# A graph layer and an attention layer on one core: transpositions behind the scalings, block sums on another engine

## The chip, the core and the metric

The kernel runs on one core of one Trainium2 chip. Times are device microseconds (us) of one execution. Engines: PE is TensorE's matmul, PEld its weight load, DVE VectorE, ACT ScalarE, POOL GpSimd, SP the engine that issues most transfers. The granted clock is the share of its full clock that TensorE was given, 1.00 being all of it. L690 is line 690 of the kernel; its code is below.

A *group* is four of the 128 batches. I measure a group from the first matmul of line 720 (attention times V) in it to the first one in the next group. Group 0 has no such matmul ahead of it; there I count from its first score matmul. Group lengths, landings and start times that are given without a fence are read from the trace's single records at these marks.

## The reference, cut to what matters

```python
x, adj: (128, 128, 512), (128, 128), float32
# layer 0
h = relu(layernorm(x))
x = x + relu(max along the row of (adj @ h) + b)  # one number per row, added to x
# layer 1
h = relu(layernorm(x))
q, k, v = h @ Wq + bq, h @ Wk + bk, h @ Wv + bv   # 512x512 weights, 8 heads of 64
weights = softmax(q k^T / 8 + mask(adj))
x = x + weights @ v
```

The kernel forms the q, k and v products by a scheme with fewer multiplications, in two levels. It needs sums of blocks of the weights (once) and of the transposed h (per group).

## The kernel before

The kernel keeps every matmul result in one of eight banks of PSUM. The parts that the argument touches (cuts marked `...`):

```python
def blocks(m):                    # DVE: 32x32 transpositions of batch m
    nc.vector.transpose(TB[g][:, :, i % 2], HN[m]...)            # L318
def move(m):                      # 16 transfers bring two batches' blocks to their place in hT
    for a in range(NQ):
        for q in range(NQ):
            nc.sync.dma_start(HT[g][...], TB[g][...])            # L328
def weight_blocks(eng, n):        # 16 sums of 128x128 blocks of weight n
    for k in (3, 2, 0, 1): ...
        eng.tensor_tensor(o, x, y, op=op)                        # L401

def scores(g):                    # 64 matmuls into all eight banks, in order
    for i in range(G):
        psc = [bank(2 * i + j)... for j in range(2)]
        for f in range(NC):
            for j in range(2):
                nc.tensor.matmul(psc[j][:, f, :], KT[g]..., QT[g]...)   # L690
        ... exp on ScalarE

def apply(g, n_last=G):           # attention times V, then the scalings
    for i in range(G):
        if i % n_last == 0:
            last = bank(7 if i == 0 else 0)      # head 7 of all four batches
        main = bank(3 + i)                       # heads 0 to 6 of batch i
        ... matmuls                              # L720
    for po, rs, oo in parts:                     # five parts: banks 3, 4, 5, 6, then 7
        nc.vector.reciprocal(rs, po[:, :, HD])                   # L737
        nc.vector.tensor_tensor(oo, po[:, :, 0:HD], rs..., op=ALU.mult)   # L738, "the scalings"

for g in range(NG):
    if g > 0:
        apply(g - 1)
    scores(g)
    part = [...]      # 18 steps: six each for the products v of group g, q and k of g + 1
    ...
    if g > 0:
        for i in range(G):
            residual(b - G + i, nc.gpsimd)       # L750, then the store
    ...               # norms of the group after next
    if g == 1: weight_blocks(nc.vector, "v")
    ...
    # in step 5: h_sum(g + 1, k), DVE differences of hT (L367), the first to read the moved blocks
    # in step 17: blocks(m + 2), blocks(m + 3), move(m + 3), the group's last two batches
    if g == 0: weight_blocks(nc.vector, "k")
```

The matmuls of `apply` fill banks 3 to 7, the scalings read them, and `scores` overwrites them a moment later.

Of the kernel before, what the change touches and what calls it, by code (L numbers as in the profile page):

```python
# [169 lines left out]
def tile_adj_preln_d2(  # L170
# [13 lines left out]
    nc = tc.nc  # L184
# [24 lines left out]
    def fast(ctx):  # L209
# [103 lines left out]
        def blocks(m):  # L313

            g, i = divmod(m, G)
            if i % 2 == 0:
                TB[g] = proj.tile([P, NQ, 2, NC, Q], F32, name="tb")
            nc.vector.transpose(  # L318
                TB[g][:, :, i % 2], HN[m].rearrange("p (c q n) -> p q c n", c=NC, q=NQ)
            )  # L320

        def move(m):

            g, i = divmod(m, G)
            if i % 2 == 1:
                for a in range(NQ):
                    for q in range(NQ):
                        nc.sync.dma_start(  # L328
                            HT[g][q * Q : (q + 1) * Q, i - 1 : i + 1, :, a * Q : (a + 1) * Q],
                            TB[g][a * Q : (a + 1) * Q, q],  # L330
                        )
# [54 lines left out]
            a = WA[n]["a21"]  # L386
            return [a[:, e // 2, e % 2 * P : (e % 2 + 1) * P] for e in range(4)]

        def weight_blocks(eng, n):


            for k in (3, 2, 0, 1):
                a = WA[n]["a22 s4 a12 s1".split()[k]].rearrange("p c (o f) -> p o c f", o=2)
                s = w_blocks(n, k)
                for o, x, op, y in (
                    (s[0], a[:, 1, 0], ALU.add, a[:, 1, 1]),
                    (s[2], s[0], ALU.subtract, a[:, 0, 0]),
                    (s[1], a[:, 0, 0], ALU.subtract, a[:, 1, 0]),
                    (s[3], a[:, 0, 1], ALU.subtract, s[2]),
                ):  # L400
                    eng.tensor_tensor(o, x, y, op=op)  # L401
# [19 lines left out]
        class Products:  # L421
# [51 lines left out]
            def add(self, out, bank, more):  # L473
                nc.vector.tensor_tensor(out, self.view(bank), self.view(more), op=ALU.add)  # L474
# [289 lines left out]
        def next_norms(m):  # L764

            return {
                0: [(norm_end, m, False), (norm_end, m + 1, False)],
                1: [(blocks, m)], 2: [(blocks, m + 1)],
                4: [(adjacency, m)], 5: [(move, m + 1)], 7: [(adjacency, m + 1), (norm_act, m + 2)],
                8: [(norm_end, m + 2), (add_bv, m), (add_bv, m + 1)],  # L770
                13: [(norm_act, m + 3)], 14: [(norm_end, m + 3)], 16: [(adjacency, m + 2)],
                17: [(blocks, m + 2), (blocks, m + 3), (move, m + 3)],
            }

        with tc.manual_schedule():

            for m in range(G):
                norm(m)
                if m < 2:
                    norm_end(m)  # L780
            transposes(0)
            transposes(1)
            norm_end(2)
            norm_end(3)
            nc.vector.tensor_single_scalar(live, adjT, 0.0, op=ALU.not_equal)
            adjacency(0)
            adjacency(1)
            transposes(2)
            transposes(3)
            weight_sums(nc.gpsimd, "v")  # L790
            plain_q(0, 0)
            weight_sums(nc.vector, "k")
            for k in range(4):
                h_sum(0, k)
            adjacency(2)
            norm(G)
            norm_end(G)
            plain_q(0, 1)
            norm(G + 1)
            norm_end(G + 1)  # L800
            adjacency(3)
            plain_q(1, 0)
            blocks(G)
            blocks(G + 1)
            move(G + 1)
            plain_q(1, 1)
            k = Products(0, "k")
            more = {
                0: [(adjacency, G), (norm, G + 2), (norm_end, G + 2)],
                1: [(norm, G + 3), (norm_end, G + 3), (blocks, G + 2)],  # L810
                2: [(adjacency, G + 1)], 3: [(blocks, G + 3), (move, G + 3)],
                4: [(adjacency, G + 2)], 5: [(adjacency, G + 3)],
            }
            for s, p in enumerate((k.p1, k.p6, k.p2, k.p7, k.p5, k.p4, k.p3)):
                p()
                for f, m in more.get(s, ()):
                    f(m)
            weight_sums(nc.gpsimd, "q")
            weight_blocks(nc.gpsimd, "q")
            for g in range(NG):  # L820
                b = g * G
# [3 lines that stand above are left out]
                part = []  # L825
                for p in [Products(g, "v")] + [Products(g + 1, n) for n in "qk" if g + 1 < NG]:
                    if p.n == "v" and g in (0, NG - 1):
                        part += [[p.p1], [p.p6], [p.p2], [p.p7], [p.p5], [p.p4, p.p3]]
                    else:
                        part += [  # L830
                            [p.p1, p.p5s], [p.p6, p.p5u], [p.p2a], [p.p43a, p.p7], [p.p5, p.p2c],
                            [p.p43b, p.p43c, p.end4, p.end3],
                        ]
                        if p.n == "v":
                            part[5] = [p.p43b]
                            late = [p.p43c, p.end4, p.end3]
                if 0 < g < NG - 1:
                    part[6] = [late[1]] + part[6] + [late[2]]
                    part[7].insert(1, lambda: h_sum(g + 1, 3))
                todo = {s: [] for s in range(len(part))}  # L840

                def add(s, *what):
                    todo[s].append(what)

                m = b + 2 * G
                if g + 1 < NG:
                    if g > 0:
                        for i in range(G):
                            residual(b - G + i, nc.gpsimd)
                    if m < B:  # L850
                        norm(m)
                        norm(m + 1)
                    else:
                        count(0, b)
                    if g == 1:
                        weight_blocks(nc.vector, "v")
                    if 0 < g < NG - 1:
                        add(0, adjacency, m - 1)
                    for k, s in enumerate((5, 5, 5, 6) if g > 0 else (4, 4, 4, 5)):
                        if 0 < g and k == 2:  # L860
                            add(s, late[0])
                        if k < 3 or g == 0:
                            add(s, h_sum, g + 1, k)
                    for k, s in ((2, 4), (3, 5), (1, 5), (0, 7)):
                        add(s, h_blocks, g + 1, k)
                    if g + 2 < NG:
                        for s, l in next_norms(m).items():
                            for what in l:
                                add(s, *what)
                    for k, s in enumerate((8, 9, 9, 10, 10, 13, 14, 15)):  # L870
                        add(s, mask, nc.gpsimd, b + k // 2, k % 2)
                    if g + 2 < NG:
                        add(0, load, 2 * g + 5)
                    if g + 3 < NG:
                        add(8, load, 2 * g + 6)
                else:
                    for k, s in enumerate((0, 0, 0, 0, 2, 2, 3, 4)):
                        add(s, mask, nc.vector, b + k // 2, k % 2)
                    for i, s in enumerate((0, 0, 0, 1)):
                        add(s, residual, b - G + i)  # L880
                for i in range(G):
                    add((2, 5, 9, 15)[i] if g + 1 < NG else i + 1, add_c, b + i)
                if g == 0:
                    weight_blocks(nc.vector, "k")
                    for i in range(G):
                        add(15, add_bv, i)
                for s, ps_ in enumerate(part):
                    for p in ps_:
                        p()
                    for f, *args in todo[s]:  # L890
                        f(*args)

            g = NG - 1
            apply(g, 2)
            count(B - 2 * G, B)
            for i in range(G):
                residual(g * G + i, nc.gpsimd if i < 2 else nc.vector)
            pc = bank(1)
            for k in range(2):
                nc.tensor.matmul(pc[0:1, 0:1], CNT[k], ones, start=k == 0, stop=k == 1)  # L900
            nc.scalar.copy(flag, pc[0:1, 0:1])
# [39 lines left out]
```

## Time and profile before

| | before |
|---|---|
| median of 4 runs (lowest to highest) | 1512.09 us (1511.21 to 1514.86) |
| span of the profiled run | 1509.5 us |
| groups 2 to 29, each | 46.27 to 46.28 us |
| group 1 | 49.88 us |
| last of the 16 late transfers of hT lands, groups 2 to 29 | 15.6 to 16.5 us into the group |
| first reader of them (DVE, L367) starts | 20.48 us into the group |

The table is read as one long repeated stretch, 28 equal groups, and a beginning with two exceptions.

### The profile page before, as it was taken

The page shows a single profiled execution, that of the slowest core. Times are in us where ns is not written, and L with a number is a line of the kernel's source. Part 1 is how long each engine was busy: PE and PEld are TensorE (multiplying, and loading weights), DVE is VectorE, ACT ScalarE, POOL GpSimd, SP SyncE. Part 2 cuts the span into 40 slices and gives each one's busy share as a digit, 9 for nine tenths or more (in the row PEclk, how much of TensorE's full clock was granted, in tenths as well). Part 3 has the DMA queues.
Part 4 walks back from the last instruction along what each step waited for, and adds up shares of the span by engine and source line. Part 5 has one row for each costly group of instructions (what it writes and reads, how often), then busy time and mean ns, then how long its engine had stood idle before and what let it go on. Part 6 is the DMA issues. An engine that isn't in the chain of part 4 may idle for free.

```text
span 1509.5 us, 36726 instructions
## 1 busy us (share of the span) xinstructions
PE 1487.0 (99%) x14013; PEld 1339.1 (89%) x14013; DVE 1188.4 (79%) x2885; ACT 596.2 (39%) x1179; POOL 973.4 (64%) x1222
## 2 busy tenths in 40 slices
PE   8999999999999999999999999999999999999997
PEld 6889989899898989888998989998899989899896
DVE  6787878878788778788787887787877878877786
ACT  3334343443344343434434443434334343443332
POOL 5767675667765676756667566766567675667760
PEclk9999999999999999999999999999999999999999
DMA  5221233222332222332223322123221233222211
GB/s 172 52 68 40 75 83 85 63 63 51 79 85 69 74 40 75 84 79 68 55 61 79 86 66 76 39 75 85 70 75 41 74 82 85 65 69 45 64 43 59
DMA packets 307826, 105.55 MB, mean 70 GB/s; under 512 B 273152, under 2 KB 273280, under 8 KB 307648
## 3 DMA queue, kind: packets, MB, share of 16 engines
q1 hardware_dynamic: 307328, 102.84, 26.9%
q8 instruction: 113, 1.85, 0.5%
q14 instruction: 65, 0.53, 0.1%
q0 software_dynamic: 176, 0.27, 0.1%
q10 hardware_dynamic: 144, 0.07, 0.0%
HBM read 37.03 MB, written 33.55 MB: 47 GB/s over the span
## 4 chain that ended last, share of the span: by engine, by line
PE 97%; DVE 2%; issue 0%; DMA 0%; POOL 0%; ACT 0%; DVEq 0%
PE bk L561 38%; PE bk L453 34%; PE bk L690 8%; PE bk L720 8%; PE bk L343 7%; PE bk L666 1%; DVE o L738 0%; DVE ssk_sb L401 0%; DVE wv_sb L401 0%; DVE st L281 0%; DMA xp<-in_x_dram 0%; PE bk L337 0%; DVE ssv_sb L401 0%; DVE c L346 0%; DVE kT L474 0%
## 5 line engine op out<-in xcount | busy, mean ns | idle before, releaser
L750 POOL TENSOR_TENSOR o<-xp,o 128x512 f32<-128x512 f32 x122 | 152.5, 1285 | 243.5 <-DVE o L738 213.6
L702 POOL TENSOR_TENSOR w<-w,live 128x512 f32<-128x512 f32 x248 | 309.1, 1275 | 0.0
L579 DVE TENSOR_TENSOR u<-u,bk 128x256 f32<-128x256 f32 x552 | 204.8, 412 | 57.8 <-PE bk L561 57.8
L698 ACT ACTIVATE w<-bk 128x512 f32<-128x512 f32 x256 | 132.0, 611 | 280.1 <-PE bk L690 276.5
L579 DVE TENSOR_TENSOR p1a<-p1a,bk 128x128 f32<-128x128 f32 x368 | 109.4, 318 | 140.0 <-ACT p1a L481 69.6
L481 ACT COPY p1a<-bk 128x512 f32<-128x512 f32 x95 | 55.6, 585 | 400.6 <-PE bk L453 399.4
L380 POOL TENSOR_TENSOR h<-hT 128x256 f32<-128x256 f32 x93 | 68.2, 733 | 196.7 <-PE bk L561 105.3
L311 POOL TENSOR_TENSOR xp<-xp,bv_sb 128x512 f32<-128x512 f32 x128 | 160.1, 1271 | 32.9 <-ACT hn L305 32.9
L690 PE MATMUL bk<-qT,kT 64*128 64x128 f32 x2048 | 138.4, 280 | 2.8
L305 ACT ACTIVATE hn<-xp,nmr,rstd 128x512 f32<-128x512 f32 x124 | 100.9, 814 | 100.9 <-POOL nmr L288 63.8
L690 PEld LDWEIGHTS bk<-qT,kT 64*128 64x128 f32 x2048 | 127.4, 187 | 10.1 <-PE bk L690 7.7
L453 PE MATMUL bk<-sv_sb,hs 128*128 128x256 f32 x512 | 131.0, 380 | 0.5 <-DVE u L492 0.5
L453 PE MATMUL bk<-hs,sk_sb 128*128 128x256 f32 x512 | 131.4, 380 | 0.0
L453 PE MATMUL bk<-hs,sq_sb 128*128 128x256 f32 x496 | 127.6, 380 | 0.0
L343 PE MATMUL bk<-hn,adjT 128*128 128x512 f32 x248 | 126.9, 593 | 0.0
L720 PE MATMUL bk<-v,w 128*64 128x65 f32 x4096 | 126.5, 222 | 0.0
L720 PEld LDWEIGHTS bk<-v,w 128*64 128x64 f32 x4096 | 122.1, 137 | 4.1 <-issue 0.3
L380 POOL TENSOR_TENSOR h<-hT,h 128x128 f32<-128x128 f32 x186 | 108.8, 585 | 14.6
L453 PEld LDWEIGHTS bk<-sv_sb,hs 128*128 128x128 f32 x512 | 90.3, 191 | 22.2 <-issue 14.3
L738 DVE TENSOR_TENSOR o<-bk,RS 128x448 f32<-128x448 f32 (+1 forms) x161 | 93.7, 582 | 7.2
L344 DVE TENSOR_REDUCE amax<-bk 128x1 f32<-128x512 f32 x128 | 87.6, 684 | 10.8 <-PE bk L343 10.8
L561 PEld LDWEIGHTS bk<-h,ssk_sb 128*128 128x128 f32 x558 | 81.8, 191 | 16.0 <-issue 14.3
(181 smaller groups left out, 3592.0 us busy)
## 6 DMA issues: line engine op xcount, KB each, us to landing
out_dram<-o SPq DMA_DIRECT2D x128, 256.0 KB, 2.3
xp<-in_x_dram SPq DMA_DIRECT2D x62, 512.0 KB, 3.9
hT<-tb SPq DMA_DIRECT2D x992, 32.0 KB, 1.9
xp<-in_x_dram SPq DMA_DIRECT2D x4, 256.0 KB, 3.5
wq_sb<-in_L_gnn_Wq_dram SPq DMA_DIRECT2D x2, 512.0 KB, 6.9
wk_sb<-in_L_gnn_Wk_dram SPq DMA_DIRECT2D x2, 512.0 KB, 9.0
wv_sb<-in_L_gnn_Wv_dram SPq DMA_DIRECT2D x2, 512.0 KB, 10.3
bv_sb<-in_L_gnn_bv_dram POOLq DMA_DIRECT2D x1, 256.0 KB, 6.4
```

The source lines that it names most:

```text
L305: nc.scalar.activation(HN[m], x_of(m), AF.Relu, scale=RSTD[m], bias=NMR[m])
L311: nc.gpsimd.tensor_tensor(x_m, x_m, bv_sb, op=ALU.add)
L343: nc.tensor.matmul(pa, adjT, HN[m], start=True, stop=True)
L380: nc.gpsimd.tensor_tensor(o, x, y, op=ALU.subtract)
L453: nc.tensor.matmul(bank[:, r, :], lhs, rhs, start=first and r == 0 and c == 0, stop=r == 1 and c == 1, skip_group_check=True,)
L561: nc.tensor.matmul(out, lhs, rhs, start=start, stop=True, skip_group_check=True)
L579: nc.vector.tensor_tensor(to, to, what, op=ALU.add)
L690: nc.tensor.matmul(psc[j][:, f, :], KT[g][r, f, i * D : (i + 1) * D], QT[g][r, f, i * D : (i + 1) * D], start=True, stop=True,)
L698: nc.scalar.activation(w[:, j], psc[j], AF.Exp, scale=HD ** -0.5)
L702: eng.tensor_tensor(w[:, j], w[:, j], live_h, op=ALU.mult)
L720: nc.tensor.matmul(pav[r, c : c + HE], w[:, h % 2, h // 2, r], V[:, i, h, :], start=True, stop=True,)
L750: eng.tensor_tensor(y, x_of(b), y, op=ALU.add)
```

## The change

Its intent: let VectorE free the attention's banks before it transposes the last two batches of a group, and take the sums of Wv away from VectorE. The sums of Wk are spread over the steps of group 0.

```diff
-        def weight_blocks(eng, n):
+        def weight_blocks(eng, n, ks=(3, 2, 0, 1)):
-            for k in (3, 2, 0, 1):
+            for k in ks:
...
-                17: [(blocks, m + 2), (blocks, m + 3), (move, m + 3)],
...
                     if g > 0:
+                        blocks(m - 2)
+                        blocks(m - 1)
+                        move(m - 1)
                         for i in range(G):
                             residual(b - G + i, nc.gpsimd)
...
-                    if g == 1:
-                        weight_blocks(nc.vector, "v")
...
                 if g == 0:
-                    weight_blocks(nc.vector, "k")
+                    for s, k in enumerate((3, 2, 0, 1)):
+                        add(s, weight_blocks, nc.vector, "k", (k,))
+                    add(4, weight_blocks, nc.gpsimd, "v", (3, 2))
+                    add(15, weight_blocks, nc.gpsimd, "v", (0, 1))
```

## The prediction

> **What bounds the kernel now.** I read the page's shares first, then the stretches of single groups, TensorE's waits, and the timelines around each wait and each boundary between groups.
>
> ```profile
> PE 1487.0 (99%) x14013; PEld 1339.1 (89%) x14013; DVE 1188.4 (79%) x2885; ACT 596.2 (39%) x1179; POOL 973.4 (64%) x1222
> ```
>
> TensorE is busy 1487.0 of 1509.5 us. The kernel handles 32 groups of four batches; from group 2 to group 29 every group takes the same time:
>
> ```profile
> 136.00:182.28 46.28, 46.19 (x442) 41.77 (x442) 36.71 (x90) 18.68 (x37) 30.41 (x38) 1.00 0.28 69
> 1015.29:1061.57 46.28, 46.19 (x442) 41.76 (x441) 36.72 (x90) 18.68 (x37) 30.41 (x38) 1.00 0.28 70
> ```
>
> Columns: length, then busy time of PE, PEld, DVE, ACT, POOL, granted clock, DMA share. TensorE works 46.19 of 46.28 us at full clock; the other engines have 9.6 us (DVE), 27.6 (ACT) and 15.9 (POOL) to spare. About 0.09 us per group is all that a better order could win there, 2.6 us over 28 groups. What else TensorE loses is in its list of waits:
>
> ```profile
> PE bk L262 <- POOL ident masks.py:199: 4.8, 1, 4.8
> PE bk L561 <- DVE p1a L579: 3.4, 2, 3.2
> PE bk L900 <- DVE live L760: 2.2, 1, 2.2
> PE bk L337 <- ACT o L305: 1.6, 1, 1.6
> PE bk L453 <- DVE u L492: 0.5, 1, 0.5
> ```
>
> The 4.8, 2.2 and 1.6 belong to start and end, which the change doesn't touch. Two are in its reach. The 3.2 us one is in group 1, where VectorE runs the 16 sums of blocks of Wv ahead of the addition that TensorE waits for:
>
> ```profile
> 95.26 0.65 DVE L401 TENSOR_TENSOR wv_sb<-sv_sb 128x128 f32<-128x128 f32 x1
> ...
> 101.17 0.28 DVE L401 TENSOR_TENSOR ssv_sb<-sv_sb,ssv_sb 128x128 f32<-128x128 f32 x1
> 101.38 0.47 DVE L579 TENSOR_TENSOR p1a<-p1a,bk 128x128 f32<-128x128 f32 x2
> 101.71 0.49 PE L561 MATMUL bk<-wv_sb,h 128*128 128x128 f32 x2 [3.23 <-DVE p1a L579]
> ```
>
> The 0.55 us one is in group 0: the 16 sums of Wk keep VectorE busy until 52.69 us, and the eviction L492 behind them frees a bank.
>
> **What the Trainium skill says.** "GPSIMD Engine Reference", section 3 (Performance versus the Vector engine), has GpSimd about twice as slow at two-input elementwise work. The trace agrees in kind: 128x128 sums have a median of 497 ns on GpSimd (the 16 of Wq), 284 ns on an undisturbed VectorE. The same page, section 1 (Specifications), says that SBUF interfaces are shared with VectorE, with contention for VectorE's instructions with two SBUF inputs. The trace agrees: Wk's sums take 430 to 540 ns while GpSimd runs its own, 280 after it stops; four cost about 1.6 us against 0.93. A transposition (one input) is unharmed: 701 ns alone, 706 under GpSimd. "DMA: Bandwidth & Descriptors", the anatomy of one DMA, has a fixed cost of about 2.0 us for the software path, mostly completion; the 32 KB transfers here, from the other path, land 1.9 us after issue. "Perfetto Trace Analysis", on identifying the most-contended engine, warns that matmul occupancy isn't distance to the roofline. So I use 99% only to see where TensorE pauses; weight loads at 89% agree that it hardly does.
>
> **The change part by part.** TensorE's instructions are the same in number and order, and so is the transfer queue's order. Only VectorE and GpSimd are reordered.
>
> (1) Transpositions behind the scalings, groups 1 to 30. VectorE at the boundary before (group 2 starts at 136.0):
>
> ```profile
> 138.09 1.29 DVE L318 STREAM_TRANSPOSE tb<-hn 128x512 f32<-128x512 f32 x2
> 139.31 0.17 DVE L737 RECIPROCAL RS<-bk 128x7 f32<-128x7 f32 x1
> ...
> 142.63 0.42 DVE L738 TENSOR_TENSOR o<-bk,RS 128x256 f32<-128x256 f32 x1
> 142.97 0.69 DVE L281 BATCH_NORM_STATS2 st<-xp 128x6 f32<-128x512 f32 x1
> ```
>
> The scalings (139.31 to 142.97, 3.66 us) move 1.22 us earlier; the transpositions move 3.66 later; from 142.97 on VectorE's order is the same. Earlier scalings free banks and let GpSimd's residuals start 1.2 us sooner, but TensorE doesn't wait for either: worth 0 to 2.6 us in all. The price is in the transfers:
>
> ```profile
> 139.41 11.68 SPq L328 DMA_DIRECT2D hT<-tb  x16
> 151.19 2.03 SPq L751 DMA_DIRECT2D out_dram<-o  x4
> 153.31 0.40 SPq L231 DMA_DIRECT2D xp<-in_x_dram  x1
> ```
>
> They start at 3.42 us of a group's time and land (single issue records) at 15.6 to 16.5. They will start at 7.08 and land at 19.2 to 20.2. First to need them is VectorE's difference of hT:
>
> ```profile
> 156.47 0.68 DVE L367 TENSOR_TENSOR hs<-hT 128x512 f32<-128x512 f32 x1
> ```
>
> That is 20.48 of the group's time. Margin 0.3 to 1.2 us where it was 4 to 5. Behind it, the third difference ends at 159.23 and TensorE's reader of it starts at 159.68, another 0.45 us. So I expect no wait of TensorE: the period stays 46.28. Stores and the load of x go out up to 3.7 us later; that load lands near 24.9 and ScalarE reads it at 24.7, but ScalarE then has 1.8 us idle.
>
> (2) Wv's sums off VectorE in group 1. The wait of 3.23 us goes. GpSimd does eight of them between 55.5 and 59.4, where it is idle 3.8 us, and eight before four additions of bv that run at 85.49: 8 x 0.46 to 0.5 = 3.7 to 4.0 us. That delays the residuals (93.26, though the scalings now end sooner) by some 1.3 us and the norms behind them, hence group 1's first transpositions by 0.2 to 0.4 us. I count 0.2 of that as felt. Part: -3.0 us.
>
> (3) Wk's sums spread over four steps of group 0. The 0.55 us wait goes. But VectorE, which worked through 46.66 to 52.69, now idles until the product of step 1 ends (about 51.2) and until ScalarE's output for the transposition (53.4, slightly sooner than 53.70). Then follow: four sums beside GpSimd's h and Wv sums (to about 55.7), the second transposition (56.4), four more contended sums (58.1), and only then L492 of the fourth product, about 58.1 to 58.8. It ran at 55.52. TensorE's sixth product overwrites that bank; without the old wait it is due at 57.35:
>
> ```profile
> 57.90 1.89 PE L453 MATMUL bk<-wv_sb,hs 128*128 128x256 f32 x8
> ```
>
> That makes a new wait of about 1.5 us. The next product waits some 0.15 us for the L474 behind the last four sums, and the late differences of hT may cost 0.1 to 0.2. Net of the 0.55: +1.2 us.
>
> Sum: 1512.4 - 3.0 + 1.2 - 0.2 (a guess at part 1) = about 1510.4 us.
>
> **The rivals.** (a) Everything saved, nothing lost: -3.8 us, 1508.6. For: VectorE has spare time in group 0, and contention may fall as sums are spread. Against: the order in part 3, which leaves VectorE idle early and busy when L492 is due. (b) The transfers become the bound: if they land later than 20.9 of a group, each 1 us costs 28 to 30 us, and 1540 (2%) is reached at 1.0 us. For: a margin of 0.3 us in the worst group, and issues that sometimes stall by 1 to 2 us near instruction fetches. Against: transpositions and issues keep their lengths, and of the spread of 15.6 to 16.5 even the worst fits. A mild form (0.1 us per group) gives 1513. (c) GpSimd becomes the bound in group 1: twice the delay I reckon is 0.5 to 1 us, 1511. (d) Earlier freed banks close the 0.09 us gaps: 1508.
>
> **Range and chances.** The parts that can be off are the new wait in group 0 (0 to 2.5 us), group 1's remainder (0 to 1), and the margin of the transfers (0 to 4 in the mild form). Runs of the kernel before spread by 3.6 us. Hence 1510.4 us, range 1507.5 to 1514.5. To be over 2% faster it would have to win 30 us, more than TensorE's whole idle time of 22.5: 1%, left for a surprise in measurement. Slower by 2% needs rival (b) in full: 2%. Within 2%: 97%.
>
> **What would show it.** In the changed profile: group 1 loses the 3.2 us wait; group 0 shows a wait of about 1.5 us of L453 for L492, near 57.4, in place of 0.55 near 53; groups 2 to 29 last 46.28 with transpositions at 5.8 us, transfers from 7.1 and landings at 19.2 to 20.2; VectorE's difference of hT still starts at 20.5 without idle time before it. I am wrong if the groups' period changes, if VectorE waits for transfers there, or if group 0 shows no new wait.

## More of the kernel before

The profile's main lines stand in the prediction. One more row, of the list of TensorE's groups of instructions, has the score matmuls: busy time, mean ns of one, and idle time ahead of them.

```profile
L690 PE MATMUL bk<-qT,kT 64*128 64x128 f32 x2048 | 138.4, 280 | 2.8
```

2.8 us of idle time is ahead of these matmuls in the whole kernel.

## The result, and the profile after

The changed kernel takes 1493.28 us (median of 4, 1492.99 to 1494.16). The ratio to the kernel before is 0.9873, 95% interval 0.9856 to 0.9891. Here and below a ratio is the mean time of one kernel's fast runs over that of the other's of the same rounds, so it isn't quite the ratio of the medians. The gain is 1.3%; at 18.8 us it is about nine times the 2 us that were predicted, and the time is far outside the range.

Where it came from, by stretches of the two profiled spans (1509.46 and 1491.72 us):

| stretch | before | after | difference |
|---|---|---|---|
| start to the first score matmul | 43.75 | 44.18 | +0.43 |
| group 0 | 42.36 | 43.22 | +0.86 |
| group 1 | 49.88 | 46.56 | -3.32 |
| groups 2 to 29 | 1295.81 | 1281.04 | -14.77 |
| group 30 | 44.15 | 43.48 | -0.67 |
| group 31 and the end | 33.51 | 33.25 | -0.26 |

The first row is no effect of the change: all kernels here are alike up to there, and this start took 43.0 to 44.7 us in their profiles. The surprise is in the repeated part, which the prediction had held constant. The stretches of groups 2, 3, 15 and 21 of the changed kernel (columns as in the prediction):

```profile
133.96:180.50 46.54, 46.07 (x442) 41.40 (x441) 36.84 (x90) 18.69 (x37) 30.20 (x38) 1.00 0.28 69
180.50:226.16 45.66, 45.66 (x441) 41.40 (x440) 36.70 (x90) 18.57 (x37) 30.51 (x39) 1.00 0.29 71
728.97:775.61 46.64, 46.08 (x441) 41.40 (x440) 36.86 (x90) 18.69 (x37) 30.20 (x38) 1.00 0.28 69
1003.95:1049.62 45.67, 45.67 (x441) 41.41 (x440) 36.70 (x90) 18.68 (x37) 30.41 (x38) 1.00 0.28 71
```

Most groups now last 45.67 us, 0.61 less than before. And TensorE's *busy* time fell with it, from 46.19 to 45.67, with the same matmuls at the same clock. Time that was "busy" before was not work. The row of the score matmuls says which:

```profile
L690 PE MATMUL bk<-qT,kT 64*128 64x128 f32 x2048 | 122.9, 275 | 0.0
```

Busy 138.4 before, 122.9 now: 15.5 us less, plus the 2.8 us of idle time, is 18.3 us, or 0.61 for each of 30 groups. The timelines of TensorE show one such run of 64, in the kernel before in groups 0, 3 and 31:

```profile
43.75 3.84 PE L690 MATMUL bk<-qT,kT 64*128 64x128 f32 x64
...
186.16 4.45 PE L690 MATMUL bk<-qT,kT 64*128 64x128 f32 x64
...
1479.83 3.84 PE L690 MATMUL bk<-qT,kT 64*128 64x128 f32 x64
```

and in the changed kernel, group 3:

```profile
184.38 3.84 PE L690 MATMUL bk<-qT,kT 64*128 64x128 f32 x64
```

In group 0 there is no `apply` ahead, no scaling to wait for, and the 64 take 3.84 us. In groups 1 to 30 they took 4.39 to 4.46. In group 31, the last, `apply` and the scalings are there, but no transpositions stand ahead of them (no group 32 is to be prepared), and the 64 take 3.84 again. The changed kernel has 3.84 everywhere. This evidence stood in the trace of before: the same 64 instructions in one kernel, with and without the transpositions ahead of the scalings.

Why the list of waits didn't show it: a matmul's record is 275 ns long on average, but 64 of them fit in 3.84 us, so each next one starts about 60 ns later and four or five overlap. A pause between two starts only becomes idle time beyond some 0.2 us. In the timeline of weight loads, which overlap less, the kernel before has its 64 in two pieces with a pause between:

```profile
186.16 3.04 PEld L690 LDWEIGHTS bk<-qT,kT 64*128 64x128 f32 x50
189.45 0.96 PEld L690 LDWEIGHTS bk<-qT,kT 64*128 64x128 f32 x14 [0.25 <-PE bk L690]
```

Bank 7 is the last to be freed; in the kernel before its scaling ends at 189.33 in this group, and the second piece begins at 189.45:

```profile
188.91 0.42 DVE L738 TENSOR_TENSOR o<-bk,RS 128x256 f32<-128x256 f32 x1
```

In the changed kernel VectorE's timeline has that scaling, then the transpositions, which the SP queue's transfers follow:

```profile
185.94 0.42 DVE L738 TENSOR_TENSOR o<-bk,RS 128x256 f32<-128x256 f32 x1
186.28 1.29 DVE L318 STREAM_TRANSPOSE tb<-hn 128x512 f32<-128x512 f32 x2
```

```profile
187.60 10.43 SPq L328 DMA_DIRECT2D hT<-tb  x16
198.13 2.02 SPq L751 DMA_DIRECT2D out_dram<-o  x4
200.24 0.41 SPq L231 DMA_DIRECT2D xp<-in_x_dram  x1
```

The transfers start 7.1 us into the group, as predicted, and land at 18.8 to 20.9. Groups 2, 6, 8, 12, 15 and 23 are longer than 45.67, by 0.02 to 0.97 us: there they land too late, at 19.95 us or later. Group 15, on VectorE:

```profile
748.52 0.41 DVE L579 TENSOR_TENSOR u<-u,bk 128x256 f32<-128x256 f32 x1
750.15 0.69 DVE L367 TENSOR_TENSOR hs<-hT 128x512 f32<-128x512 f32 x1 [1.22 <-issue]
```

The releaser is printed as "issue", but the last transfer landed 0.27 us before the difference of hT starts, at 749.88; VectorE had waited for it, 1.22 us, of which TensorE lost 0.97 (in group 6 it is 0.43 and 0.17). Over the 28 groups this costs 1281.04 - 28 x 45.67 = 2.3 us: 17.1 won, 2.3 given back, 14.8 left.

TensorE's list of waits after the change, whole:

```profile
PE bk L262 <- POOL ident masks.py:199: 4.8, 1, 4.8
PE bk L903 <- DVE live L760: 2.2, 1, 2.2
PE bk L337 <- ACT o L305: 1.8, 1, 1.8
PE bk L561 <- PE bk L453: 1.0, 2, 0.6
PE bk L453 <- DVE u L492: 0.9, 1, 0.9
PE bk L561 <- DVE p1a L579: 0.2, 1, 0.2
```

The 3.2 us wait is gone, and the new one for L492 in group 0 is there, 0.9 us. The reader should see what this list does *not* have: no line in it or in the one of before is worth 17 us.

### The profile page after: what moved, and what is told of

The parts are those of the page before. It is cut to its first block, busy times and chain, and to the rows that moved or that the text cites. A ratio compares the mean times of both kernels' runs of the same rounds, so it can differ in the third digit from the quotient of the medians.

```text
span 1491.7 us, 36725 instructions
## 1 busy us (share of the span) xinstructions
PE 1473.7 (99%) x14013; PEld 1328.7 (89%) x14013; DVE 1184.1 (79%) x2869; ACT 595.8 (40%) x1179; POOL 978.0 (66%) x1238
## 4 chain that ended last, share of the span: by engine, by line
PE 96%; POOL 2%; DVE 1%; issue 1%; ACT 0%; DMA 0%; DVEq 0%; POOLq 0%
PE bk L561 38%; PE bk L453 33%; PE bk L720 8%; PE bk L690 8%; PE bk L343 7%; PE bk L666 1%; POOL ssq_sb L401 0%; POOL o L750 0%; POOL xp L311 0%; POOL h L380 0%; DMA xp<-in_x_dram 0%; POOL rstd L286 0%; DVE ssk_sb L401 0%; PE bk L337 0%; POOL sq_sb L413 0%
## 5 line engine op out<-in xcount | busy, mean ns | idle before, releaser
L698 ACT ACTIVATE w<-bk 128x512 f32<-128x512 f32 x256 | 128.8, 628 | 275.0 <-PE bk L690 275.0
L690 PE MATMUL bk<-qT,kT 64*128 64x128 f32 x2048 | 122.9, 275 | 0.0
L690 PEld LDWEIGHTS bk<-qT,kT 64*128 64x128 f32 x2048 | 116.8, 188 | 2.5 <-issue 0.3
```

The source lines that it names most:

```text
L690: nc.tensor.matmul(psc[j][:, f, :], KT[g][r, f, i * D : (i + 1) * D], QT[g][r, f, i * D : (i + 1) * D], start=True, stop=True,)
L698: nc.scalar.activation(w[:, j], psc[j], AF.Exp, scale=HD ** -0.5)
```

## The experiments

My theory after the result: the last 16 score matmuls wait for bank 7 (and 6), which the scalings free; two transpositions ahead of the scalings (1.22 us) delay that by 0.61 us more than TensorE has slack. The rivals: TensorE doesn't wait there and the sums matter; the gain comes from the residuals and stores, which start earlier too; every delay costs in proportion. The first four kernels ran on one chip, the next four on another, the last three on a third. All results were correct. Unless said otherwise the time is the median of 4 runs. The diffs are shortened to the lines that matter.

**Only the transpositions moved** (e1_transp_only), on the kernel before:

```diff
-                17: [(blocks, m + 2), (blocks, m + 3), (move, m + 3)],
+                        blocks(m - 2); blocks(m - 1); move(m - 1)     # ahead of the residuals
```

> The kernel before with the transpositions moved behind the scalings and nothing else. Theory (the score matmuls wait, unseen in the list of waits, for the banks that the scalings free): every group from 1 to 30 is 0.61 us shorter where the transfers land in time, 45.67 us, the 64 score matmuls take 3.84 us instead of 4.45; in all about -16 us, near 1496 us. Rival (the theory of the prediction: TensorE doesn't wait there, and the sums of Wv and Wk make the difference): at most -0.2 us, near 1512 us.

1494.34 us, ratio 0.9881 (0.9864 to 0.9897). Groups of 45.67, scores in 3.84. This part alone makes 17.3 us, nearly the whole gain; the prediction's reading of it is refuted.

**Only the sums of Wv moved** (e2_wv_only), on the kernel before:

```diff
-                    if g == 1: weight_blocks(nc.vector, "v")
+                    add(4, weight_blocks, nc.gpsimd, "v", (3, 2))
+                    add(15, weight_blocks, nc.gpsimd, "v", (0, 1))
```

> The kernel before with the sums of Wv on GpSimd in group 0 and nothing else. Both theories: the wait of 3.2 us in group 1 goes, the groups from 2 on stay at 46.28 us; -3.0 to -3.3 us, near 1509 us. If the sums of Wv had a part in the other groups, their period would fall below 46.28 us.

1507.63 us, ratio 0.9971 (0.9954 to 0.9987). Groups 2 to 29 stay at 46.27 to 46.28; group 1 falls from 49.88 to 46.56. Group 0 is 42.35, as before (42.36). The time is 1.4 us lower than expected; the span to the first score matmul was 0.75 us shorter in this profile, which the edit doesn't touch.

**Only the sums of Wk spread** (e3_wk_only), on the kernel before:

```diff
-                    weight_blocks(nc.vector, "k")
+                    for s, k in enumerate((3, 2, 0, 1)):
+                        add(s, weight_blocks, nc.vector, "k", (k,))
```

> The kernel before with the sums of Wk spread over four steps of group 0 and nothing else. Theory: group 1 starts about 1.0 us later, since a wait for the eviction L492 of about 0.8 us takes the place of 0.55 us and the differences of hT come later; groups from 2 on 46.28 us; +0.5 to +1.3 us. Rival (spreading helps): -0.5 us.

My expectation failed in both ways. Group 0 got shorter, 42.13 us, and no wait for L492 is left: alone, spreading helps a little. Yet the time was 1513.06 us, ratio 1.0 (0.9983 to 1.0016). In the profiled run, one of 1514.01 us, group 1 took 52.55 us. The wait of 3.23 us is still in group 1 of this kernel, and behind it TensorE ran at half clock. The stretches around it (the column after POOL's is the granted clock), of this run:

```profile
98.00:101.00 3.00, 0.78 (x4) 0.35 (x2) 2.93 (x11) 0.91 (x2) 2.67 (x5) 1.00 0.31 52
101.00:108.00 7.00, 5.99 (x24) 5.64 (x25) 4.14 (x14) 1.61 (x3) 0.00 (x0) 0.51 0.71 239
```

and of the kernel before, whose profiled run has the same wait:

```profile
101.00:108.00 7.00, 6.29 (x43) 5.74 (x44) 6.35 (x19) 2.24 (x4) 0.00 (x0) 1.00 0.71 233
```

24 matmuls in 7 us against 43. So a run with this wait may or may not pay a second time. Taken over all runs whose clock is on record, those of the kernels that hold the 3.2 us wait (the kernel before and this one) had a mean clock of 0.996 to 0.998 and took 1510.6 to 1515.0 us, each one above 1513 at 0.996; the runs of e2_wv_only, of e9_weights_both and of the changed kernel, without it, had 0.998 or 0.999 and stay within 1.9 us of each other, kernel by kernel. e1_transp_only, with a wait of 2.5 us left there, lies between (0.997 and 0.998). That the pause causes the low clock is not shown: one trace alone has both, with the clock low from 101.09 to 107.92 us and the pause up to 102.01.

**One transposition ahead, one behind** (e4_one_ahead), on the changed kernel:

```diff
                 if g > 0:
+                    if g + 1 < NG:
+                        blocks(b + 2 * G - 2)
                     apply(g - 1)
...
-                        blocks(m - 2)
```

> The changed kernel with the first of the two transpositions (0.62 us) ahead of the scalings again, the second behind. Theory (a bank is waited for once the scalings are later than TensorE by more than a slack; two transpositions of 1.22 us in all cost 0.61, so the slack is 0.61): the period stays at 45.67 to 45.70 us, within 1 us of the changed kernel, 1493 to 1494.5 us. Rival (every delay of the scalings costs in proportion): half is lost, 45.97 us, near 1502 us.

1494.22 us, ratio 0.9881 (0.9864 to 0.9897). Most groups last 45.68 us. Half the delay costs 0.01 us a group, the whole of it 0.61: there is a threshold, as with a slack, and no proportion.

**Both transpositions ahead of the last scaling only** (e5_before_last_bank), on the changed kernel:

```diff
             for j, (po, rs, oo) in enumerate(parts):
+                if j == len(parts) - 1 and ahead is not None:
+                    ahead()                       # blocks(m - 2), blocks(m - 1)
                 nc.vector.reciprocal(rs, po[:, :, HD])
```

> The changed kernel with both transpositions between the fourth and the fifth scaling: only the last bank is freed late, and the residuals, which need the fifth scaling too, start as late as in the kernel before. Theory (the last bank freed sets when the last 16 score matmuls start): the period is back at 46.28 us, about 1509 to 1511 us, and the score matmuls take 4.45 us. Rival (the early start of most scalings makes the gain): four fifths of it stay, near 1497 us.

1509.24 us, ratio 0.997 (0.9954 to 0.9987); groups 46.27 to 46.28, scores 4.45. Four of five scalings are as early as in the changed kernel and nothing of the gain in these groups is left. The residuals start as late as in the kernel before here (7.14 us of a group), so this run alone leaves them as a rival; the next one takes them out, and with both, bank 7 is what sets the period. Here TensorE's list of waits names the cause, though it still counts a fraction of it (4.5 us of 29 x 0.61 = 17.7):

```profile
PE bk L690 <- DVE o L740: 4.5, 29, 0.2
```

(L740 is the scaling's line in this kernel.)

**Residuals late** (e6_residual_late), on the changed kernel; the sums repeat values that are there already:

```diff
                         move(m - 1)
+                        nc.gpsimd.tensor_tensor(dum, O[g - 1][:, G - 1, N - 1 : N], mhalf, op=ALU.mult)
+                        for _ in range(2):
+                            nc.gpsimd.tensor_tensor(w_blocks("q", 0)[0], a22[:, 1, 0], a22[:, 1, 1], op=ALU.add)
```

> The changed kernel with 1.1 us of idle work on GpSimd between the scalings and the residuals, so that residuals, norms and stores start about as late as in the kernel before, while the banks are freed early. Theory of the banks: the period stays 45.67 us, within 1 us of the changed kernel, 1492.5 to 1494.5 us. Rival (residuals and what hangs on them, not banks): the gain goes, near 1510 us.

1495.08 us, ratio 0.9877 (0.986 to 0.9894). The residuals start at 7.04 us of a group (before: 7.14, changed kernel: 5.95), so the delay is restored; most groups last 45.74, 0.07 more than 45.67. The rival of the residuals would have asked for 46.28. The median is 0.6 us above the range I gave: group 1 took 47.68 (46.56 in the changed kernel), and groups 2 to 29 together 0.9 us more.

**Each transposition twice** (e7_transp_twice), on the changed kernel:

```diff
                         blocks(m - 1)
+                        again(m - 2)     # same instruction, same output
+                        again(m - 1)
                         move(m - 1)
```

> The changed kernel with each of the two transpositions done twice (same result), so that the transfers of hT start and land 1.25 us later while the scalings keep their place. Theory (landings after about 19.9 us of a group are paid for by TensorE one to one, as some groups of the changed kernel show): every group waits, 0.65 us on average where it was 0.08; +14 to +18 us, 1507 to 1511 us. Rival (the transfers are hidden): within 1 us of the changed kernel.

1510.01 us, ratio 0.9978 (0.9961 to 0.9995). The scores still take 3.84 us; VectorE now waits for the transfers in every one of groups 2 to 29, and these together are 1296.62 us, 15.6 more than in the changed kernel. Its list of waits has the line

```profile
DVE hs L374 <- DMA hT<-tb: 22.6, 23, 1.8
```

(L374 is L367 there; in the changed kernel this wait is 2.4 us in 4 places, plus 1.7 us in 3 put down to issue.) The transfers start at 8.29 us of a group in place of 7.11, and these 1.2 us eat up nearly the whole gain. The transfers are not hidden any more: their margin is used up.

**A version in gaps** (e8_in_gaps), on the changed kernel: the transpositions go into two gaps of VectorE, in the last step of the q products and in that of the k products; Wk's sums fill VectorE's idle time in group 0, and twelve of Wv's sixteen GpSimd's.

```diff
-                        blocks(m - 2); blocks(m - 1); move(m - 1)
+                if g + 2 < NG:
+                    m3 = b + 2 * G + 2
+                    part[11].insert(1, lambda: blocks(m3))
+                    part[17].insert(1, lambda: (blocks(m3 + 1), move(m3 + 1)))
...
-                    for s, k in enumerate((3, 2, 0, 1)):
-                        add(s, weight_blocks, nc.vector, "k", (k,))
-                    add(4, weight_blocks, nc.gpsimd, "v", (3, 2))
-                    add(15, weight_blocks, nc.gpsimd, "v", (0, 1))
+                    add(0, weight_blocks, nc.vector, "k", (3, 2))
+                    todo[1].insert(0, (weight_blocks, nc.vector, "k", (0,)))
+                    add(3, weight_blocks, nc.vector, "k", (1,))
+                    add(4, weight_blocks, nc.gpsimd, "v", (3, 2, 0))
+                    add(15, weight_blocks, nc.gpsimd, "v", (1,))
```

> A version meant to beat both: the two transpositions in gaps of VectorE during the products of q and k, so that the boundary holds none and the transfers start before it; in group 0 the sums of Wk in VectorE's idle time ahead of the first evictions, three quarters of Wv's sums in GpSimd's idle time. Theory: all groups at 45.67 us with no wait for transfers (-2.3 us), group 0 and 1 1 to 1.5 us shorter; 1489 to 1490.5 us. Rival (the transpositions in the gaps hold up evictions): +0.1 to 0.6 us per group, 1493 to 1507 us.

1488.02 us, ratio 0.9834 (0.9818 to 0.985), 1 us better than expected. Every one of groups 1 to 29 lasts 45.67 or 45.68 us; the late transfers land before 13.4 us; group 0 is 41.90. A stretch of it (group 2):

```profile
131.29:176.96 45.67, 45.67 (x441) 41.40 (x441) 36.76 (x90) 18.58 (x37) 30.45 (x38) 1.00 0.29 70
```

and one of the gaps on VectorE's timeline, 1.06 us long in the other kernels, with the transposition in it and 0.44 left:

```profile
175.93 0.70 DVE L318 STREAM_TRANSPOSE tb<-hn 128x512 f32<-128x512 f32 x1
177.07 0.75 DVE L579 TENSOR_TENSOR u<-u,bk 128x256 f32<-128x256 f32 x2 [0.44 <-PE bk L561]
```

**Both moves of the sums, transpositions as before** (e9_weights_both): the changed kernel with step 17 put back and the three lines at the boundary removed.

> The kernel before with both moves of the sums (Wv to GpSimd, Wk spread) and the transpositions left ahead of the scalings. Theory (each move alone costs group 0 nothing, 42.35 and 42.13 us from the first score matmul to the end of the group, but together they contend and bring it to 43.2 us, as in the changed kernel): group 0 43.2 us, group 1 near 47.2 us (46.56 plus 0.6 for the scalings), groups from 2 on 46.28 us; about -2 us, 1509 to 1510.5 us. Rival (the transpositions' place makes group 0 longer): group 0 42.1 to 42.4 us and -3 us.

1509.07 us, ratio 0.9979 (0.9962 to 0.9995). Group 0 takes 43.25 us, where each move alone gave 42.35 and 42.13. So the loss in group 0 belongs to the two moves together. In the changed kernel's trace, Wk's second to fourth quarters run at 54.1 to 59.8 us, and GpSimd's first Wv sums at 55.4 to 59.2, with single sums of 420 to 545 ns on VectorE while both are at it; in e3_wk_only, where GpSimd has no Wv sums, the third quarter takes 244 to 292 ns a sum. Group 1 took 46.56, not the 47.2 I expected: it is 46.55 to 46.56 in e2_wv_only, here and in the changed kernel, wherever the transpositions are. Something other than bank 7 sets group 1 in these. I had suspected GpSimd's later norms, and the traces bear it out. GpSimd's last eight Wv sums delay its residuals in group 1, which start at 7.88 us of the group in the changed kernel, where e1_transp_only, without these sums, has 5.96. e6_residual_late puts them 1.10 later (8.98) and group 1 grows by 1.12, to 47.68; e8_in_gaps, with only four late sums, has 6.77 and the group is at 45.67, like the others. So in the changed kernel Wv's late sums still cost 0.89 us once.

**The changed kernel and the version in gaps again, side by side** (after_again, e8_again), without an edit.

> The changed kernel again, beside the version with the transpositions in gaps on the same chip: 1493 to 1494 us, groups of 45.67 us with waits for the transfers in 5 to 9 of 28 groups.

> The version with the transpositions in gaps again, beside the changed kernel on the same chip: 1487.5 to 1489 us, 5 us below the changed kernel; every group 45.67 us.

1492.51 us (1492.22 to 1492.78), ratio 0.987 (0.9853 to 0.9886), and 1488.64 us (1488.47 to 1488.81), ratio 0.9845 (0.9828 to 0.9861). The changed kernel is 0.5 us below my range; VectorE waits for the transfers in six of the 28 groups, and three of these are clearly longer (45.85, 46.33 and 46.87 us). The version in gaps beats it by 3.9 us here, less than the 5 I had written; its groups are all at 45.67.

## Why the prediction was wrong

By its own steps:

- **What bounds the kernel** (TensorE, 46.28 us per group, "all that a better order could win there" 0.09 us): the first half held, the second failed. Busy time had been taken for work. The prediction quoted the skill's warning that matmul occupancy isn't distance to the roofline, and then used it as just that. 0.52 us of each group's 46.19 "busy" us were pauses between overlapping records; with the 0.09 of idle time they are the 0.61.
- **Part 1** (transpositions behind the scalings, "TensorE doesn't wait for either: worth 0 to 2.6 us in all"): this is the step that failed. In its place e1_transp_only shows about 17 us, e5_before_last_bank that the wait is for bank 7, and e6_residual_late that the residuals have next to no part in it. The term of -0.2 us should have been -15.4 (groups 2 to 30, after what the transfers take back). Two of its own three signs of being wrong came true: the groups' period changed, and VectorE waited for transfers.
- **Part 1, the transfers**: right in kind and nearly in numbers. Start 7.08 predicted, 7.11 measured; landings of 19.2 to 20.2 predicted, 18.8 to 20.9 measured. The difference of hT was to start at 20.48 without idle time; since the scores are 0.61 us shorter it is due at 19.87, and six groups pay for that. The landing from which lateness costs was put at 20.9; it is about 19.9 in the changed kernel (group 23 lands at 19.95 and pays 0.02 us). The "slope" of rival (b), 1 us for 1 us, was borne out: group 15 lands at 20.91 in the changed kernel and at 21.51 in e7_transp_twice, and lasts 46.64 and 47.24. (Its 2% line is 1542.6 us, not 1540; nothing hangs on that.)
- **Part 2** (Wv's sums, -3.0 us): right. Group 1 lost 3.32 us in e2_wv_only, and stays 0.28 above the next groups there (0.2 was counted).
- **Part 3** (Wk's sums, +1.2 us): right in sign and mechanism. A wait for L492 of 0.9 us in place of 0.55 was seen (1.5 was predicted), and group 0 grew by 0.86. That it takes both moves to bring it about (e3_wk_only, e9_weights_both) was implied in the working, which had the contention in it, but in my expectation for e3_wk_only I forgot it.
- **Rivals**: (d), that earlier freed banks close gaps, had the right cause and a size of 2.6 us instead of 17, for the same misreading. (a), nothing lost, is refuted by the 0.86 us of group 0. (c), GpSimd as the bound of group 1, held: with the banks freed early it costs the 0.89 us told under e9_weights_both.
- **Range and chances**: 97% for "within 2%" was right, but the bound of "22.5 us of idle time" behind it was unsound: 15.5 us more lay in the score matmuls alone, counted as busy. A gain over 22.5 us was possible: the version in gaps (e8_again) has 23.6 us against the kernel before on one chip (1488.64 and 1512.25).

## What to carry to other kernels

Where a pipelined engine's records overlap, compare how long the same run of instructions takes with and without the suspected wait in front of it, before trusting idle time: here groups 0 and 31 had the answer, 3.84 us against 4.45. Order an engine's work at a boundary by who waits for its results; what nobody waits for goes behind, or better into a gap where the engine is idle anyway, since moving it behind spends the margin of whatever follows it. Two moves that are each harmless can collide when they put work on two engines at the same time.

## What the Trainium skill lacked or had wrong

- "Perfetto Trace Analysis", summary of the profiler's window by engine: it says that TensorE's end is estimated, and the section on the most-contended engine that matmul busy time misleads because instructions look smaller. Here they look larger together: a repeated wait of 0.61 us appeared as 0.09 us of idle time (2.8 us of 18.3 in all), and weight loads showed a pause of 0.25. No page says to compare equal runs of matmuls by their length (3.84 and 4.45 us), which finds it.
- "PSUM — Partial Sum Buffer": no figure that I found for what a bank costs that is freed late by another engine; the runs show a threshold (0.62 us of delay free, 1.22 us cost 0.61).
- "TensorE: Matmul & The Clock Gate", part 1: half rate after an idle window of about 3.4 us. The runs agree roughly and only sometimes: the same pause of 3.23 us went with 6.8 us of clock 0.5 in one profile (e3_wk_only, group 1 2.67 us longer than before) and by none in another (the kernel before).
- "GPSIMD Engine Reference", section 3: about 2 times slower. Here 497 against 284 ns for 128x128 sums (1.75 times; 450 to 460 for Wv's last eight in the changed kernel, 1.6 times) and 1285 against 685 ns for 128x512 residuals (1.9 times); its note on contention for two SBUF inputs agrees (430 to 540 ns against 284).
- "DMA: Bandwidth & Descriptors", anatomy of one DMA: a fixed 2.0 us, given there for the software path. The median of the 32 KB transfers here, on the other path, is 1.9 us, but landings of 16 in a row scatter by 2.1 us from group to group (18.8 to 20.9), and it is this scatter, not the median, that cost time. What makes it was not tested. In the changed kernel's trace the groups that land at 18.8 have their 16 issues without a gap; groups 2, 6, 8 and 12 have one of 1.5 to 2.1 us between two issues, with a transfer of the instruction queue within 0.2 us of its start, and in group 15 single transfers take up to 3.7 us to land.
